# A scan that starts from the tile of the chunk before: one VectorE copy per chunk removed, two halves exchanged, one load moved

## The chip, the cores and the metric

The kernel runs on one core of a Trainium2 chip. The metric is the device time of one execution in microseconds (us). The core has a matrix engine (PE, with its weight loads shown apart as PEld), VectorE (DVE), ScalarE (ACT), GpSimd (POOL), and a queue of SyncE (SP) that only issues DMA transfers here. Each engine takes its own instructions in order; between engines, and between an engine and a DMA, waits go through semaphores.

## The reference

The input is eight images of 128 x 128 points with 128 channels. A first layer (linear attention with a residual) and the front of a second (a projection to 256 channels, a 3x3 depthwise convolution, SiLU) are not touched by the change. What matters is the selective scan after them. For four directions of walking over an image (rows, rows backwards, columns, columns backwards), and for each of the 256 channels and 16384 points in walking order:

```python
def step(xc, inp):
    dlt, dut, Bt, Ct = inp
    dA = jnp.exp(dlt[..., None] * A[:, None])
    xc = dA * xc + dut[..., None] * Bt[:, :, None, :]
    y = jnp.einsum('kbcn,kbn->kbc', xc, Ct)
    return (xc, y)
```

The state has one number per channel, so `y = xc * C`. The four directions are brought back to natural order and added up, gated with SiLU(z), normalized over the channels and projected to 128 channels.

## The kernel before

The program has three stages, one after the other: `layer0`, `layer1_front` and `layer1_scan`. Only `layer1_scan` is changed. It begins about 4870 us after the start.

**Units.** The output images are handled one after the other, eight in all. Each has four sweeps (a `Slot`; its `place` is 0 to 3), one for each direction, and each sweep is cut into 16 chunks of 1024 points. One chunk of one sweep is a unit: there are 512, numbered by n. The 256 channels stand in two halves c = 0, 1 of 128 partitions, so that a unit's data are a tile `ubt` of 128 x 2 x 1024 fp32 numbers (1 MB), loaded from DRAM by `load(n)`. There are four such buffers.

**Work on a unit.** `delta` (PE) makes the step sizes in a PSUM tile `px`, `soften` (ACT) takes their softplus into `sp`, `decay` (ACT) the exponential back into `px`, `weigh` (POOL) multiplies `ubt` by `sp` in place. `scan` (VectorE, L899 backwards and L901 forwards) runs the recurrence over the 1024 points of each channel half, in place in `ubt`. Its starting value is a pointer to a column of a small tile `state`, or 0.0 for the first chunk of a sweep. `state` (L909) fills that tile: a VectorE reduction with one element per channel, that is, a copy of the last element of each half of `ubt` (column 1023, or column 0 when the sweep walks backwards). `spread` (PE) makes C in PSUM for each half of 512 points.

**Adding up.** The sum over directions stands in a big SBUF tile `y`. In a sweep of place 0, `emit` (L927) writes h * C straight into `y`, in two halves of 512 points. In places 1 to 3, `emit` for the first half writes h * C into PSUM (L939, L943), `gather` (L951) adds that to `y`, and `emit` for the second half multiplies `ubt` in place (L932); POOL adds that half to `y` in `add` (L958). Once `emit` has overwritten a half of `ubt`, the scan's own value is gone from it, which is why the state is copied.

**Order.** `step(n)` writes out the order of all engines by hand, and the context `in_order` keeps it. On VectorE, one step is: emit, gather and emit of unit n-1, then `scan(n, 0)`, `scan(n, 1)`, `state(n)`. During the place-0 sweep of images 1 to 7, the image before leaves as well ("leaving"): two gates (multiplications with z, one on VectorE, one on POOL, L978), squares, moments and projection (PE), `variance` (L1011) behind `state`, and `store` (L1029), eight small VectorE instructions between the two scans that fill two buffers `r`; each `r` goes out by a 256 KB DMA of SP (L1033). In the same steps and those around them, POOL starts DMAs that add a 1 MB block of DRAM to `y` (L854).

**Queue of SP.** In a place-0 step it issues, in this order: four small loads of `rows` for unit n+2 (L863, L864), `load(n + 3)` (L870), two loads of z (L974) and the two stores of `r` (L1033). In places 1 to 3 `load(n + 3)` stands at the end of the step. `load(n + 3)` overwrites the buffer of unit n-1, so it waits until that has been read for the last time: by `emit(n - 1, 1)` in place 0, by `add(n - 1)` in the others.

Of the kernel before, what the change touches and what calls it, by code (L numbers as in the profile page):

```python
# [8 lines left out]
F32 = mybir.dt.float32  # L9
BF16 = mybir.dt.bfloat16  # L10
AF = mybir.ActivationFunctionType
ALU = mybir.AluOpType
AX = mybir.AxisListType
# [3 lines left out]
P = 128  # L17
B = 8
H = W = 128
L = H * W  # L20
NH, HD = 4, 32
NC2 = 2
# [8 lines left out]
CH = 1024  # L31
CW = CH // H
NCH = L // CH
# [664 lines left out]
def layer1_scan(ctx: ExitStack, tc, ubs, xps, zs, gs, dtw, dtb, a_log, gamma, beta, w_out, out):  # L698
# [15 lines left out]
    nc = tc.nc  # L714
# [3 lines left out]
    sm = ctx.enter_context(tc.tile_pool(name="l2s", bufs=4))  # L718
# [34 lines left out]
    for i in range(3):  # L753
        t = const.tile([P, CH], BF16, name=f"rows{i}")
# [3 lines left out]
    for i in range(3):  # L758
        t = const.tile([P, D2], BF16, name=f"dtw{i}")
# [20 lines left out]
    for j in range(2):  # L780
        for hf in range(2):
            at = 32 * (2 * j + hf)
# [19 lines left out]
    class Slot:  # L802


        def __init__(self, n, o, s):
            self.o, self.s = o, s
            self.b, self.k = o // 4 + 2 * s, o % 4
            self.back = self.k % 2 == 1
            self.order = NAT if self.k >= 2 else TURN
            self.dt_image, dt_dir = 2 * self.k + self.b // 4, self.b % 4  # L810
            self.dt_order = NAT if dt_dir >= 2 else TURN
            self.dt_turned_back = self.back != (dt_dir % 2 == 1)
            self.y_turned = (self.order == TURN) != (s >= 2)
            self.y_back = s % 2 == 1
            self.place = n % K
            self.dw = dws[n % 3]

        def weights(self):
# [24 lines left out]
    units = []  # L843
    for o in range(B):
        for s in ([3, 0, 1, 2] if o % 4 < 2 else [1, 2, 3, 0]):
            sl = Slot(len(units) // NCH, o, s)
            units += [(sl, i) for i in range(NCH)]

    ubt, sp, da, st = {}, {}, {}, {}

    def add_d(o, m):

# [3 lines left out]
    def load_rows(n):  # L856
        sl, i = units[n]
        m = sl.at(i)
        rw = rws[n % 3]
        md = NCH - 1 - m if sl.dt_turned_back else m  # L860
        src = xps[sl.dt_image, sl.dt_order].rearrange("j r l -> (j r) l")
        for j in range(3):
            nc.sync.dma_start(rw[3 * NR * j : 3 * NR * j + 3 * NR, :], src[:, md * CH : md * CH + CH])  # L863
        nc.sync.dma_start(rw[96:99, :], xps[sl.b, sl.order, :, R + 1, m * CH : m * CH + CH])  # L864

    def load(n):
        sl, i = units[n]
        m = sl.at(i)
        ubt[n] = wp.tile([P, NC2, CH], F32, name="ubt", tag="ub", bufs=4)
        nc.sync.dma_start(ubt[n], ubs[sl.b, sl.order].rearrange("c p l -> p c l")[:, :, m * CH : m * CH + CH])  # L870
# [16 lines left out]
    def decay(n, c):  # L887
        sl, i = units[n]
        nc.scalar.activation(da[n, c], sp[n, c], AF.Exp, scale=sa[:, sl.s, c : c + 1])  # L889
# [4 lines left out]
    def scan(n, c):  # L894
        sl, i = units[n]
        x, e = da[n, c], ubt[n][:, c, :]
        start = 0.0 if i == 0 else st[n - 1][:, c : c + 1]
        if sl.back:
            nc.vector.tensor_tensor_scan(e[:, ::-1], x[:, ::-1], e[:, ::-1], start, ALU.mult, ALU.add)  # L899
        else:  # L900
            nc.vector.tensor_tensor_scan(e, x, e, start, ALU.mult, ALU.add)  # L901

    def state(n):
        sl, i = units[n]
        st.pop(n - 1, None)
        if i < NCH - 1:
            st[n] = t = sm.tile([P, NC2], F32, name="state")
            at = 0 if sl.back else CH - 1
            nc.vector.tensor_reduce(t, ubt[n][:, :, at : at + 1], AX.X, ALU.max)  # L909

    cps, ts = {}, {}

    def spread(n, hf, tag):
        cps[n, hf] = p = pe.tile([P, 1, GN], F32, name="pc", tag=tag)
        nc.tensor.matmul(p[:, 0, :], csel, rws[n % 3][:, hf * 512 : hf * 512 + 512], start=True, stop=True)  # L915

    def emit(n, hf):

        sl, i = units[n]
        h = ubt[n][:, :, hf * 512 : hf * 512 + 512]
        c = cps.pop((n, hf)).to_broadcast([P, NC2, GN])
        if sl.place == 0:
            v = sl.y_at(i, hf)
            split = "p c (a b) -> p c a b"
            nc.vector.tensor_tensor(v, h.rearrange(split, b=H), c.rearrange(split, b=H), ALU.mult)  # L927
            if hf == 1:
                ubt.pop(n)
            return  # L930
        if hf == 1:
            nc.vector.tensor_tensor(h, h, c, ALU.mult)  # L932
            return
        p = da.pop((n, 1))
        if sl.y_turned:
            ts[n] = p.rearrange("p (c b a) -> p c b a", c=NC2, a=GW)
            t = p.rearrange("p (c b a) -> p c a b", c=NC2, a=GW)
            split = "p c (a b) -> p c a b"
            nc.vector.tensor_tensor(t, h.rearrange(split, b=H), c.rearrange(split, b=H), ALU.mult)  # L939
        else:  # L940
            t = p.rearrange("p (c q) -> p c q", c=NC2)
            ts[n] = t.rearrange("p c (a b) -> p c a b", b=H)
            nc.vector.tensor_tensor(t, h, c, ALU.mult)  # L943

    def gather(n):

        sl, i = units[n]
        v = sl.y_at(i, 0)
        if sl.y_turned:
            v = v.rearrange("p c a b -> p c b a")  # L950
        nc.vector.tensor_tensor(v, v, ts.pop(n), ALU.add)  # L951

    def add(n):
        sl, i = units[n]
        h = ubt.pop(n)[:, :, 512:].rearrange("p c (a b) -> p c a b", b=H)
        v = sl.y_at(i, 1)
        for c in range(NC2):
            nc.gpsimd.tensor_tensor(v[:, c], v[:, c], h[:, c], ALU.add)  # L958

# [10 lines left out]
    def fetch(o, m):  # L970
        for hf in range(2):
            zt[m, hf] = z = wp.tile([P, NC2, GN], F32, name="z", bufs=6)
            p = mirrored(o, m, hf)
            nc.sync.dma_start(z, zs[o].rearrange("c p l -> p c l")[:, :, p * GN : p * GN + GN])  # L974

    def gate(o, m, hf, eng):
        z, ym = zt[m, hf], piece(m, hf)
        eng.tensor_tensor(z, ym[:, :, ::-1] if o % 2 == 1 else ym, z, ALU.mult)  # L978

    def square(m, hf):  # L980
        nc.scalar.activation(piece(m, hf), zt[m, hf], AF.Square)  # L981
# [57 lines left out]
    for o in range(B):  # L1039
        n = (o + 1) * K * NCH  # L1040
# [11 lines left out]
    N = len(units)  # L1052

    def step(n):
        live = 0 <= n < N
        then = n + 1 < N
        before = 1 <= n <= N
        now, last, soon, later = (leaving.get(n + i) for i in (0, -1, 1, 2))
        first = before and units[n - 1][0].place == 0
        if before:  # L1060
            emit(n - 1, 0)
            if not first:
                gather(n - 1)
        if now and last:
            gate(*now, 1, nc.vector)
        if before:
            emit(n - 1, 1)
        if n + 2 < N:
            load_rows(n + 2)
        if first and n + 3 < N:  # L1070
            load(n + 3)
        if n in fetched:
            fetch(*fetched[n])
        if live:
            decay(n, 0)
        if now:
            square(now[1], 1)
        if live:
            decay(n, 1)
            weigh(n, 0)  # L1080
        if last:
            deviation(last[1])
        if live:
            weigh(n, 1)
        if now:
            moments(now[1])
        if live:
            scan(n, 0)
            da.pop((n, 0))
        if last:  # L1090
            for hf in range(2):
                store(*last, hf)
        if then:
            for c in range(NC2):
                delta(n + 1, c)
        if now:
            keep(now[1])
        if then:
            soften(n + 1, 0)
        if now:  # L1100
            to_tokens(now[1])
            square_mean(now[1])
        if then:
            soften(n + 1, 1)
        if live:
            scan(n, 1)
            state(n)
        if now:
            variance(now[1])
        if live:  # L1110
            spread(n, 0, "pc")
            spread(n, 1, "pt")
        if soon and now:
            gate(*soon, 0, nc.gpsimd)
        elif soon:
            gate(*soon, 1, nc.gpsimd)
        elif later:
            gate(*later, 0, nc.gpsimd)
        if soon:
            square(soon[1], 0)  # L1120
        if now:
            p = da.pop((n, 1)) if live else px.tile([P, CH], F32, name="px")
            for hf in range(2):
                project(now[1], hf, p[:, hf * 512 : hf * 512 + 512])
        elif live and units[n][0].place == 0:
            da.pop((n, 1))
        if before and not first:
            add(n - 1)
        if n + 3 < N and not first:
            load(n + 3)  # L1130
        if n in weighed:
            units[weighed[n]][0].weights()
        if n in summed:
            add_d(*summed[n])
# [78 lines left out]
```

## Time and profile before

| what | value |
|---|---|
| time, median of 3 runs | 9600.28 us (9591.18 to 9600.95) |
| profiled execution: its time, and its span | 9596.25 us, 9594.5 us |
| VectorE busy | 8167.1 us, 85% of the span |
| POOL, ACT, PE busy | 7188.9 us, 7164.4 us, 6323.6 us |
| both scan lines with a state pointer | 480 + 480 instructions, 2336 ns each, 2211 us |
| `state`, L909 | 480 instructions, 155 ns each, 74.5 us |
| `ubt` loads, L870 | 512 DMAs of 1 MB |

A group of instructions in the profile has its line, engine and operation, the tiles it writes and reads, the shapes and the count; behind the first bar the busy time and the mean time of one; behind the second the engine's idle time before them, with what ended most of it. Busy times of VectorE overlap: an instruction that waits for nothing begins some 80 ns before the end of the one in front, so the pitch from start to start, not the duration, says what an instruction costs. Durations and waits are those of the profiled execution.

### The profile page before, as it was taken

Reading aid. Unit: us, or ns where it says so; the run is one execution under the profiler, and the core shown is the slowest. Engines: PE = TensorE matmul, PEld = TensorE weight load, DVE = VectorE, ACT = ScalarE, POOL = GpSimd, SP = SyncE. Lnnn points to the kernel's source line nnn. Section 1 sums busy time; section 2 is a strip of 40 time slices with the busy share of each in tenths; the row PEclk is TensorE's granted clock in tenths of the full one; section 3 lists DMA queues with packets and bytes.
Section 4 is the critical chain, followed back from the end, with each engine's and each line's share of the span. In section 5 each row is a group of like instructions: output and inputs, shape, how many; then the busy total and the mean of one; then the engine's idle time right before and its main releaser. Section 6 shows DMA issues by size and latency. Waiting matters only on the chain. (4 is left out here: it accounts for less than half of the span.)

```text
span 9594.5 us, 89820 instructions
## 1 busy us (share of the span) xinstructions
PE 6323.6 (66%) x24190; PEld 3144.2 (33%) x24352; DVE 8167.1 (85%) x8668; ACT 7164.4 (75%) x8256; POOL 7188.9 (75%) x4361
## 2 busy tenths in 40 slices
PE   8999998988977788777823544636345363543636
PEld 5555655554322233222300311304023040220403
DVE  6667765563988899888989999999999999999996
ACT  5556565566877788777878888887887888788785
POOL 3445544455665578776859999998998999999897
PEclk9999999999988899888955755757556575665857
DMA  2332233313476678987765957769486685867858
GB/s 91 133 133 83 92 132 132 132 75 135 172 262 233 227 262 248 266 264 265 248 199 166 271 164 216 229 177 263 150 237 203 185 259 164 242 190 198 242 165 212
DMA packets 1034807, 1851.21 MB, mean 193 GB/s; under 512 B 274852, under 2 KB 500772, under 8 KB 1026112
## 3 DMA queue, kind: packets, MB, share of 16 engines
q1 hardware_dynamic: 999488, 1711.23, 54.2%
q0 software_dynamic: 34816, 134.23, 7.1%
q8 instruction: 199, 3.26, 0.1%
q14 instruction: 304, 2.49, 0.1%
HBM read 1153.03 MB, written 692.12 MB: 192 GB/s over the span
## 5 line engine op out<-in xcount | busy, mean ns | idle before, releaser
L892 POOL TENSOR_TENSOR ubt<-ubt,sp 128x1024 f32<-128x1024 f32 x1024 | 2457.5, 2456 | 197.3 <-ACT sp L885 107.8
L881 PE MATMUL px<-rows,dtw 128*128 128x512 bf16 x1893 | 914.6, 576 | 2259.8 <-DVE y L951 1032.6
L516 POOL TENSOR_TENSOR tap<-tap 128x1024 f32<-128x1024 f32 x512 | 1206.0, 2366 | 634.7 <-ACT tap L514 511.8
L524 DVE SCALAR_TENSOR_TENSOR acc<-xb,cw,acc 128x1024 f32<-128x1024 f32 x1024 | 1320.7, 1290 | 52.7 <-ACT tap L514 0.9
L885 ACT ACTIVATE sp<-px 128x1024 f32<-128x1024 f32 x1024 | 1044.2, 1024 | 398.3 <-PE px L881 244.5
L958 POOL TENSOR_TENSOR y<-y,ubt 128x512 f32<-128x512 f32 x768 | 1164.2, 1568 | 138.0 <-DVE ubt L932 135.1
L506 PE MATMUL acc<-xi,wt 128*128 128x512 f32 x2048 | 953.9, 609 | 384.6 <-ACT ures L531 384.2
L881 PEld LDWEIGHTS <-dtw 128*128 128x128 bf16 x2048 | 164.8, 110 | 3054.1 <-issue 951.5
L889 ACT ACTIVATE px<-sp,sa 128x1024 f32<-128x1024 f32 x1024 | 1110.2, 1109 | 6.1
L899 DVE TENSOR_TENSOR_SCAN ubt<-px,state,ubt 128x1024 f32<-128x1024 f32 x480 | 1106.2, 2336 | 6.6 <-issue 4.9
L901 DVE TENSOR_TENSOR_SCAN ubt<-px,state,ubt 128x1024 f32<-128x1024 f32 x480 | 1105.0, 2336 | 6.5 <-issue 4.7
L514 ACT ACTIVATE tap<-xb,cw 128x1024 f32<-128x1024 f32 x768 | 834.0, 1139 | 68.4 <-POOL tap L516 67.9
L885 ACT ACT_TABLE_LOAD x512 | 656.9, 1283 | 185.3 <-PE px L881 149.8
L282 POOL TENSOR_TENSOR q<-q,qs 128x512 f32<-128x512 f32 x256 | 271.2, 1060 | 642.2 <-DVE qs L281 642.2
L506 PEld LDWEIGHTS acc<-xi,wt 128*128 128x128 f32 x2048 | 383.9, 192 | 929.8 <-ACT ures L531 486.7
L889 ACT ACT_TABLE_LOAD x512 | 656.9, 1283 | 9.1
L1023 PEld LDWEIGHTS px<-wg,z 128*128 128x128 f32 x4096 | 586.7, 229 | 132.2 <-issue 126.4
L1023 PE MATMUL px<-wg,z 128*128 128x128 f32 x4096 | 585.6, 312 | 0.0
L915 PE MATMUL pc<-rows,csel 128*128 128x512 bf16 x1017 | 516.3, 588 | 100.8 <-DVE rstd L1011 91.8
L479 PE MATMUL pxb<-xi,wi 128*128 128x512 f32 x1024 | 495.9, 606 | 4.3 <-ACT xb L488 4.3
L951 DVE TENSOR_TENSOR y<-y,px 128x1024 f32<-128x1024 f32 x384 | 468.6, 1220 | 14.2
L298 ACT ACTIVATE sq<-o 128x512 f32<-128x512 f32 x256 | 161.2, 630 | 423.0 <-DVE o L296 421.8
(158 smaller groups left out, 15369.2 us busy)
## 6 DMA issues: line engine op xcount, KB each, us to landing
ubt<-ubs SPq DMA_DIRECT2D x512, 1024.0 KB
zs<-z SPq DMA_DIRECT2D x512, 256.0 KB
ubs<-ures SPq DMA_DIRECT2D x256, 512.0 KB
ubs<-turned SPq DMA_DIRECT2D x256, 512.0 KB
z<-zs SPq DMA_DIRECT2D x256, 512.0 KB
y<-gs POOLq DMA_DIRECT2D x128, 1024.0 KB, 12.0
rows<-xps SPq DMA_DIRECT2D x1536, 60.0 KB
xi<-x SPq DMA_DIRECT2D x120, 576.0 KB
```

What stands on the lines that cost most here:

```text
L506: nc.tensor.matmul(acc[:, s, :], wt[:, j, c, :], x, start=(j == 0), stop=(j == len(ON_PE) - 1))
L514: nc.scalar.activation(t, at(n, c, *d), AF.Copy, scale=cw[:, c, tap(*d) : tap(*d) + 1])
L516: nc.gpsimd.tensor_tensor(sums[n, c], sums[n, c], t, ALU.add)
L524: nc.vector.scalar_tensor_tensor(acc, at(n, c, *d), cw[:, c, tap(*d) : tap(*d) + 1], acc, ALU.mult, ALU.add)
L881: nc.tensor.matmul(p[:, hf * 512 : hf * 512 + 512], sl.dw[:, c * P : c * P + P], src, start=True, stop=True)
L885: nc.scalar.activation(t, da[n, c], AF.Softplus)
L889: nc.scalar.activation(da[n, c], sp[n, c], AF.Exp, scale=sa[:, sl.s, c : c + 1])
L892: nc.gpsimd.tensor_tensor(ubt[n][:, c, :], ubt[n][:, c, :], sp.pop((n, c)), ALU.mult)
L899: nc.vector.tensor_tensor_scan(e[:, ::-1], x[:, ::-1], e[:, ::-1], start, ALU.mult, ALU.add)
L901: nc.vector.tensor_tensor_scan(e, x, e, start, ALU.mult, ALU.add)
L958: nc.gpsimd.tensor_tensor(v[:, c], v[:, c], h[:, c], ALU.add)
L1023: nc.tensor.matmul(po[:, w, :], z[:, c, w * H : w * H + H], wg[:, c, :], start=(c == 0), stop=(c == NC2 - 1))
```

## The change

Four edits that belong together. The scan's starting value is now read from `ubt` of the unit before, at its last element, so `state` and its tile go. That element must then survive until `scan(n, 1)`: the half of `ubt` that holds it must not be overwritten in place, so in places 1 to 3 of a forward sweep the halves change roles: half 1 goes through PSUM and `gather`, half 0 is multiplied in place and added by POOL (`first` is the number of the half that goes to PSUM). In backward sweeps the last element is in half 0, and nothing is exchanged. The order of `emit` and of `spread` follows. Finally the buffer of unit n-1 is free later: in a place-0 step `load(n + 3)` moves behind `scan(n, 1)`, and so behind the z loads and the two stores in SP's queue; in the others it stays at the end of the step and waits for `scan(n, 1)` besides `add(n - 1)`.

```diff
+            self.first = 1 if self.place and not self.back else 0
...
     def scan(n, c):
-        start = 0.0 if i == 0 else st[n - 1][:, c : c + 1]
+        last = 0 if sl.back else CH - 1
+        start = 0.0 if i == 0 else ubt[n - 1][:, c, last : last + 1]
...
-    def state(n):
-        sl, i = units[n]
-        st.pop(n - 1, None)
-        if i < NCH - 1:
-            st[n] = t = sm.tile([P, NC2], F32, name="state")
-            at = 0 if sl.back else CH - 1
-            nc.vector.tensor_reduce(t, ubt[n][:, :, at : at + 1], AX.X, ALU.max)
...
     def emit(n, hf):
-            if hf == 1:
-                ubt.pop(n)
             return
-        if hf == 1:
+        if hf != sl.first:
             nc.vector.tensor_tensor(h, h, c, ALU.mult)
             return
...
     def gather(n):
-        v = sl.y_at(i, 0)
+        v = sl.y_at(i, sl.first)
...
     def add(n):
-        h = ubt.pop(n)[:, :, 512:].rearrange("p c (a b) -> p c a b", b=H)
-        v = sl.y_at(i, 1)
+        hf = 1 - sl.first
+        h = ubt[n][:, :, hf * 512 : hf * 512 + 512].rearrange("p c (a b) -> p c a b", b=H)
+        v = sl.y_at(i, hf)
...
     def step(n):
-            emit(n - 1, 0)
+            half1 = units[n - 1][0].first
+            emit(n - 1, half1)
...
-            emit(n - 1, 1)
+            emit(n - 1, 1 - half1)
         if n + 2 < N:
             load_rows(n + 2)
-        if first and n + 3 < N:
-            load(n + 3)
...
             scan(n, 1)
-            state(n)
+        if first:
+            ubt.pop(n - 1)
+            if n + 3 < N:
+                load(n + 3)
...
-            spread(n, 0, "pc")
-            spread(n, 1, "pt")
+            half1 = units[n][0].first
+            spread(n, half1, "pc")
+            spread(n, 1 - half1, "pt")
...
         if before and not first:
             add(n - 1)
+            ubt.pop(n - 1)
```

More of the change, by code (lines that the diff above doesn't have):

```diff
@@ L847, in layer1_scan @@
             units += [(sl, i) for i in range(NCH)]
-    ubt, sp, da, st = {}, {}, {}, {}
+    ubt, sp, da = {}, {}, {}
     def add_d(o, m):
```

## The prediction

> **What bounds the kernel now.** I read the page's totals first, then VectorE's waits in the scan stage, its timeline where a sweep ends, and the timelines of VectorE and SP where it stalls.
>
> ```profile
> PE 6323.6 (66%) x24190; PEld 3144.2 (33%) x24352; DVE 8167.1 (85%) x8668; ACT 7164.4 (75%) x8256; POOL 7188.9 (75%) x4361
> L909 DVE TENSOR_REDUCE state<-ubt 128x2 f32<-128x2 f32 x480 | 74.5, 155 | 16.5
> ```
>
> VectorE is the busiest engine, and in the scan stage it is 95% busy (4502.55 of 4724 us in the window from 4870 us). What the change removes looks like 91 us there: 480 copies with 74.5 us of busy time and 16.5 us of idle time before them. Whether that is real is seen at the last chunk of a sweep, where no copy is made. VectorE's timeline has such a chunk behind an ordinary one:
>
> ```profile
> 5680.47 4.58 DVE L899 TENSOR_TENSOR_SCAN ubt<-px,state,ubt 128x1024 f32<-128x1024 f32 x2
> 5685.09 0.15 DVE L909 TENSOR_REDUCE state<-ubt 128x2 f32<-128x2 f32 x1
> 5685.16 1.22 DVE L939 TENSOR_TENSOR px<-ubt,pc 128x1024 f32<-128x1024 f32 x1
> 5686.42 1.22 DVE L951 TENSOR_TENSOR y<-y,px 128x1024 f32<-128x1024 f32 x1
> 5687.55 1.21 DVE L932 TENSOR_TENSOR ubt<-ubt,pc 128x1024 f32<-128x1024 f32 x1
> 5688.69 4.58 DVE L899 TENSOR_TENSOR_SCAN ubt<-px,state,ubt 128x1024 f32<-128x1024 f32 x2
> 5693.37 1.23 DVE L939 TENSOR_TENSOR px<-ubt,pc 128x1024 f32<-128x1024 f32 x1
> 5694.64 1.22 DVE L951 TENSOR_TENSOR y<-y,px 128x1024 f32<-128x1024 f32 x1
> 5695.77 1.21 DVE L932 TENSOR_TENSOR ubt<-ubt,pc 128x1024 f32<-128x1024 f32 x1
> 5696.90 4.46 DVE L899 TENSOR_TENSOR_SCAN ubt<-px,ubt 128x1024 f32<-128x1024 f32 x2
> ```
>
> From scan to scan it is 8.22 us with the copy (5680.47 to 5688.69) and 8.21 without (5688.69 to 5696.90). The scans end at 5685.05 and 5693.27; with a copy, emit starts 0.11 us after that, without one 0.10. The first instruction that reads the scan's result has to wait for its end. If that is the copy, its own pitch of 0.07 us covers the rest of emit's start; if it is emit, which waits for VectorE and for PE, it starts that much later by itself. Over all chunks of places 1 to 3 the median period is 8.213 us with and 8.221 us without a copy. The copy is hidden.
>
> The stalls of VectorE are elsewhere. Its waits from 4870 to 9451 us, the longest in total first:
>
> ```profile
> DVE r L1029 <- DMA out<-r: 38.0, 25, 3.4
> DVE ubt L901 <- POOL ubt L892: 19.6, 5, 14.4
> DVE rstd L1011 <- ACT mv L1007: 16.1, 35, 1.5
> ```
>
> All 25 of the first row are in place-0 steps: the store wants a buffer `r` whose DMA of a step ago has not landed. The longest one, on VectorE and then in SP's queue:
>
> ```profile
> 7233.23 2.33 DVE L901 TENSOR_TENSOR_SCAN ubt<-px,state,ubt 128x1024 f32<-128x1024 f32 x1
> 7238.98 2.16 DVE L1029 SCALAR_TENSOR_TENSOR r<-px,rstd,bw 128x128 f32<-128x128 f32 x8 [3.42 <-DMA out<-r]
> ```
>
> ```profile
> 7222.24 0.38 SPq L870 DMA_DIRECT2D ubt<-ubs  x1
> 7222.73 1.02 SPq L974 DMA_DIRECT2D z<-zs  x2
> 7225.40 1.41 SPq L1033 DMA_DIRECT2D out<-r  x2
> ```
>
> The stores issued at 7225.40 stand behind 1 MB of `ubt`, issued 3.2 us earlier. In the packet records of this stretch the 4096-byte packets of `ubt` run until 7228, those of z until about 7230, and the 512-byte ones of the stores begin then. At 7231 POOL's accumulating DMA starts, takes about 45 packets per us until 7237, and the store ends only with it.
>
> **The skill.** The Trainium skill, "VectorE: DVE Perf Modes", section "The DRAIN you can't avoid", says that a read after a write on the same engine needs a semaphore, and that a semaphore costs nothing extra there. The trace agrees with the first and not with the second: an instruction without such a wait starts about 83 ns before the end of the one in front, the copy 34 ns after the scan's end, and emit, when it waits itself, 104 ns after it. "DMA: Bandwidth & Descriptors", section "Queues, rings and completion order", says that descriptors of a ring are taken in order and that an engine alternates between rings packet by packet. The packet records above agree. "SBUF — State Buffer", section "SBUF: two separate sides", has a VectorE operation with two SBUF inputs and a GpSimd one exclude each other: the gate (L978) takes 1.2 us or about 2.2 us, the longer where it overlaps a `weigh`.
>
> **The change part by part.** Copies, places 1 to 3: 8 images x 3 sweeps x 15 = 360, each +8 ns (8.221 - 8.213): +3 us. Copies in place 0 of images 1 to 7, 105 of them: `variance`, which does not read the scan, stands behind the copy. With a copy, the pitches of second scan, copy, `variance` and emit are 2374 + 73 + 73 + 1128 = 3648 ns; at the sweep's last chunk, without a copy, those of scan, `variance` and emit are 2257 + 186 + 1138 = 3581. That is -67 ns, -7 us in all, if VectorE bounds those steps. Image 0's 15 in place 0 have no `variance`: nothing.
>
> The pointer: the scan reads one column per channel half as before; 2336 ns with a pointer against 2281 without, so nothing changes. The exchange of halves: the same shapes, counts and neighbours on VectorE, PE and POOL: nothing; if the addresses mattered, it would show in 180 forward steps at most.
>
> The load in places 1 to 3: it is issued when `add(n - 1)` ends, 1.1 us (median) before the second scan ends (1.8 in place 3), so it goes out that much later. Behind it in SP's queue are the next step's `rows` loads, which wait for `spread` on PE and come about 0.7 us later, a whole step before they are used. The least time between a `ubt` landing and its `weigh` is 5.5 us in the records. Nothing; without that cover each us late would be a us on the path.
>
> The load in place 0 moves by 6.6 us (median; 10.1 at most), past two z loads and two stores. It landed 5.8 us after issue (median; 9.3 at most), and `weigh` came at least 16.8 us after that in images 1 to 7, 12.4 in image 0, where the move is 4.5 us. At least 6.7 us of margin remains. The stores now have only z and the `ubt` of the step before ahead of them. The 1 MB that leaves their way is 256 packets at 159 ns over 16 engines, 2.5 us, and up to 6 us at the rate left beside POOL's DMA. The stalls are 0.3 to 3.4 us, so most should go.
>
> What that is worth: 23 steps with such a stall last 13.06 us on average, the other 75 of chunks 1 to 14 last 11.14 (from scan starts). 23 x 1.92 = 44 us; this counts the waits that follow a stall (0.4 us for `mv`, 0.6 before the next scan) and the gate, which is mostly the short one after a stall. I take 70% of it, -31 us, since the 16 DMA engines are busy for 0.91 to 0.93 of all these sweeps, so other queueing will remain; the ends are 0 and all of 44. The 28 us of the same wait after 9451 us stay: there are no `ubt` loads any more.
>
> Sum: +3 - 7 - 31 = -35 us. The profiled execution took 9596.25 us (span 9594.5), the median is 4 us above. From 9600 that gives 9565 us.
>
> **The rivals.** (a) Likeliest, as above: 9540 to 9581, chance 0.64. (b) The stores are late for another reason (their own 512-byte packets, POOL's DMA), and only the copies' +3 and -7 us remain: 9596, within 0.2%. For it speaks that the three sweeps whose stores go out in 512-byte packets (images 3, 4, 7) hold 16 of the 23 stalled steps; against it that `ubt` packets are seen in front of the store. 0.20. (c) The copies were on the path after all: emit, waiting itself, starts as early as the copy did. Then 480 x 73 ns = 35 us more go, and 9530 results, or 9474 if all 91 us of the row went. The last chunks of all sweeps speak against it. 0.05. (d) Slower. The transfers of SP's queue use eight completion semaphores in turn, and a transfer waits for the one eight places ahead of it. With nine transfers in a place-0 step, the second store now waits for the `ubt` load of the step before to land; before, the last `rows` load did. The store comes about 8 us after that load's issue. While a load lands within 8 us it costs nothing; at the 9.3 us seen at most, plus 2 us of landing, the store is late by some 3 us, and so is `r`. If this happened in a third of the 105 steps, 35 x 3 = +105 us, less the 35 gained: 9670; at 20 steps it about balances. Slower by over 0.2%: 0.11.
>
> **How the numbers follow.** 0.2% (19 us) is about what a measurement of this kernel can tell from no change. Faster: (a) and (c), 0.69; same 0.20; slower 0.11. The range takes in all but (c)'s larger end and (d): 9535 to 9606; the likeliest case's own is 9540 to 9581.
>
> **What would show it.** Right: periods in places 1 to 3 of 8.22 us, emit starting 0.10 us behind the scan; the wait of `r` for its store down from 38 to about 10 us before 9451 us; place-0 sweeps of images 3, 4 and 7 down from 188.1, 191.6 and 186.0 us to about 180; no new wait of `weigh` for `ubt`. Wrong: periods near 8.14 us (c); the same waits of `r` (b); the second store held by a `ubt` landing, or longer gates because POOL now collides with them (d).

## The result

The changed kernel takes 9560.44 us (median of 6 runs, 9557.33 to 9567.8) against 9591.68 us of the kernel before (6 runs, 9581.65 to 9600.95). The ratio is 0.9968, with a 95% interval of 0.9957 to 0.9979: faster by 0.32%, or 31 us. The prediction said 9565 us, and faster.

The page of the changed kernel, its totals by engine and the group of one of the two scan lines:

```profile
PE 6331.1 (66%) x24352; PEld 3113.6 (33%) x24352; DVE 8131.2 (85%) x8188; ACT 7168.0 (75%) x8256; POOL 7193.5 (75%) x4361
L904 DVE TENSOR_TENSOR_SCAN ubt<-px,ubt 128x1024 f32<-128x1024 f32 x512 | 1176.5, 2330 | 25.4 <-POOL ubt L894 19.6
```

VectorE has 480 instructions fewer (8668 to 8188), but its busy time falls by only 36 us, not by the 74.5 us of the row that went: of a copy's 155 ns, the last 83 lay under the start of emit, and 480 x 72 ns is 35 us. The scans that start from a column of `ubt` cost what they did with a pointer to `state`: 2334 ns, 2336 before (the 2330 of the line has the 32 in it that start from 0.0).

The timeline of VectorE at the place where the copy was seen to be hidden, a chunk of places 1 to 3:

```profile
5674.97 4.58 DVE L902 TENSOR_TENSOR_SCAN ubt<-px,ubt 128x1024 f32<-128x1024 f32 x2
5679.66 1.23 DVE L932 TENSOR_TENSOR px<-ubt,pc 128x1024 f32<-128x1024 f32 x1
...
5683.19 4.58 DVE L902 TENSOR_TENSOR_SCAN ubt<-px,ubt 128x1024 f32<-128x1024 f32 x2
```

No copy, and from scan to scan still 8.22 us (5674.97 to 5683.19). The scan ends at 5679.55 and emit begins 0.11 us later, as it did behind the copy. The median over all chunks of places 1 to 3 is 8.221 us; it was 8.213 with the copy.

The waits of VectorE between 4870 and 9415 us, where the last scan ends:

```profile
DVE r L1023 <- DMA out<-r: 29.3, 17, 3.9
DVE ubt L904 <- POOL ubt L894: 19.6, 5, 14.5
DVE rstd L1005 <- ACT mv L1001: 17.1, 23, 1.7
```

The first row was 38.0 us in 25 waits. It fell by much less than the prediction took for its mechanism, and yet the time came out as predicted. Where the time went is seen in the seven sweeps of place 0 in which an image leaves. From first scan to first scan of the next sweep they took 175.6, 179.5, 188.1, 191.6, 180.1, 181.6 and 186.0 us, in all 1282.4; now 176.0, 176.9, 179.8, 181.6, 178.5, 178.7 and 179.2, in all 1250.8. That is -31.7 us, most of it where the prediction saw it, in images 3, 4 and 7, for which it had forecast about 180. The whole scan stage, first scan to last, became 29.5 us shorter, so everything outside these sweeps became some 2 us longer; the prediction had +3 us for places 1 to 3. (The profiled execution is 36.8 us shorter than that of before, since the two stages ahead, which nobody touched, ended 6.7 us earlier in it.)

The waits of SP's queue in the scan stage show the two things that the change added there, waits for the scan and for a landed `ubt`:

```profile
SPq L872 <- DVE ubt L904: 1025.5, 195, 7.7
...
SPq L1027 <- DMA ubt<-ubs: 173.5, 68, 5.3
```

The last row is the rival (d) of the prediction: 68 times the queue stood at the second store, for up to 5.3 us, until the `ubt` load of the step before had landed. Counted from when the store's `r` was full, 60 stores went out late for it, by 2.2 us on average. Before, the row had one wait, of 0.9 us. The mechanism exists, then; whether it costs anything is the question of one of the experiments.

### The profile page after: what moved, and what is told of

Read it like the earlier page. It is cut to its first block, busy times and chain, and to the rows that moved or that the text cites. A ratio compares the mean times of both kernels' runs of the same rounds, so it can differ in the third digit from the quotient of the medians.

```text
span 9557.7 us, 89859 instructions
## 1 busy us (share of the span) xinstructions
PE 6331.1 (66%) x24352; PEld 3113.6 (33%) x24352; DVE 8131.2 (85%) x8188; ACT 7168.0 (75%) x8256; POOL 7193.5 (75%) x4361
## 5 line engine op out<-in xcount | busy, mean ns | idle before, releaser
L883 PE MATMUL px<-rows,dtw 128*128 128x512 bf16 x2048 | 952.9, 565 | 2234.3 <-DVE y L944 1062.6
L904 DVE TENSOR_TENSOR_SCAN ubt<-px,ubt 128x1024 f32<-128x1024 f32 x512 | 1176.5, 2330 | 25.4 <-POOL ubt L894 19.6
L902 DVE TENSOR_TENSOR_SCAN ubt<-px,ubt 128x1024 f32<-128x1024 f32 x512 | 1178.0, 2331 | 12.3 <-POOL ubt L894 6.1
L1017 PEld LDWEIGHTS px<-wg,z 128*128 128x128 f32 x4096 | 560.5, 220 | 118.8 <-issue 113.7
L1017 PE MATMUL px<-wg,z 128*128 128x128 f32 x4096 | 560.8, 303 | 0.0
```

The source lines that it names most:

```text
L883: nc.tensor.matmul(p[:, hf * 512 : hf * 512 + 512], sl.dw[:, c * P : c * P + P], src, start=True, stop=True)
L1017: nc.tensor.matmul(po[:, w, :], z[:, c, w * H : w * H + H], wg[:, c, :], start=(c == 0), stop=(c == NC2 - 1))
```

## Experiments

Theory 1: the moved load is the whole gain, because 1 MB leaves the way of the stores. Rivals: the gain is in the copies; or the stores are late by themselves and the loads' place is indifferent.

### The moved load alone

The kernel before, with its copies and its halves; in a place-0 step the load goes behind the second scan. It still waits only for `emit`, so that it is issued as soon as the two stores ahead of it are.

```diff
         if n + 2 < N:
             load_rows(n + 2)
-        if first and n + 3 < N:
-            load(n + 3)
...
             scan(n, 1)
             state(n)
+        if first and n + 3 < N:
+            load(n + 3)
```

> The kernel before with one edit: in place-0 steps the load of unit n+3 stands behind the stores in SP's queue; the copies and the halves stay. Theory 1 (the moved load is what saves, because the stores no longer stand behind 1 MB): 15 to 30 us less than the kernel before, place-0 sweeps of images 1 to 7 near 180 us, waits of r for its store below 38 us. Theory 2 (the copies are what saves): no change, 0 to -5 us, sweeps as before.

Measured: 9552.59 us, ratio 0.9964 (0.9950 to 0.9977) to the 9588.11 us of the kernel before beside it. For the gain, no copy has to go and no halves have to change roles. VectorE's wait of `r` for its store, to the end of the last scan:

```profile
DVE r L1029 <- DMA out<-r: 17.2, 10, 2.8
```

The sweeps of place 0 come to 1243.2 us, even below the changed kernel's 1250.8.

### The rest of the change alone

The changed kernel in places 1 to 3, and place 0 as before: the copy kept there, and the load ahead of the stores.

```diff
-        start = 0.0 if i == 0 else ubt[n - 1][:, c, last : last + 1]
+        start = 0.0 if i == 0 else ubt[n - 1][:, c, last : last + 1] if sl.place else st[n - 1][:, c : c + 1]
...
+        if first:
+            ubt.pop(n - 1)
+            if n + 3 < N:
+                load(n + 3)
         if n in fetched:
             fetch(*fetched[n])
```

> The changed kernel with the copy kept in place 0 and the load there at its old spot; in places 1 to 3 no copy and the halves exchanged. Theory 1: the 360 copies were hidden, +3 us against the kernel before, periods of 8.221 us, emit 104 ns behind the scan. Theory 2: 360 x 73 ns = 26 us less. The same run bounds what exchanging the halves and the later load in places 1 to 3 do: nothing by theory 1.

Measured: 9589.98 us, ratio 1.0002 (0.9994 to 1.0011). The 360 copies, the exchanged halves and the later load of places 1 to 3 are worth nothing, and rival (c) falls. Its wait of `r` is 43.1 us in 28 waits, its sweeps of place 0 come to 1272.4 us.

### A second copy

If one copy is hidden under emit's start, a second one should not be. The kernel before with the reduction done twice, its second result unread.

```diff
             nc.vector.tensor_reduce(t, ubt[n][:, :, at : at + 1], AX.X, ALU.max)
+            t2 = sm.tile([P, NC2], F32, name="state2", bufs=1)
+            nc.vector.tensor_reduce(t2, ubt[n][:, :, at : at + 1], AX.X, ALU.max)
```

> The kernel before with a second copy of the state behind the first, which nothing reads. Theory 1 (one copy fills the time that emit would need anyway after the scan's end): the second one costs its whole pitch, 73 ns x 480 = +35 us, periods of 8.286 us in places 1 to 3. If a copy is free whatever stands there (VectorE not the bound): 0 us. If a copy costs its busy time: +74 us.

Measured: 9609.26 us, ratio 1.0027 (1.0018 to 1.0036), +26 us. VectorE's timeline:

```profile
5667.29 4.58 DVE L899 TENSOR_TENSOR_SCAN ubt<-px,state,ubt 128x1024 f32<-128x1024 f32 x2
5671.91 0.16 DVE L909 TENSOR_REDUCE state<-ubt 128x2 f32<-128x2 f32 x1
5671.98 0.15 DVE L911 TENSOR_REDUCE state<-ubt 128x2 f32<-128x2 f32 x1
5672.05 1.22 DVE L941 TENSOR_TENSOR px<-ubt,pc 128x1024 f32<-128x1024 f32 x1
```

Emit now starts 0.18 us behind the scan's end at 5671.87, and the median period is 8.275 us against 8.213: the second copy costs 62 ns, most of its pitch of 70. The first is free, the second is paid. That settles why the busy time of the copies was worth nothing in places 1 to 3.

### The load between z and the stores

If it is the stores that must not stand behind 1 MB, then moving the load behind the z loads only, still ahead of the stores, gains nothing. The kernel before with:

```diff
-        if first and n + 3 < N:
-            load(n + 3)
         if n in fetched:
             fetch(*fetched[n])
+        if first and n + 3 < N:
+            load(n + 3)
```

> The kernel before with the load of a place-0 step moved only half of the way: behind the two z loads, still ahead of the two stores. Theory 1 (what counts is 1 MB in the ring ahead of the stores): nothing gained, within 10 us of the kernel before, waits of r for its store 30 us or more. Rival (what counts is that z lands earlier, or that the load comes later at all): most of the gain of the load moved the whole way, some 30 us.

Measured: 9651.44 us, ratio 1.0059 (1.0046 to 1.0072) to 9592.52 us: not the same but 59 us slower. The waits of 30 us or more came, the time within 10 us did not; the rival's gain did not come either. The waits of VectorE from 4870 to 9400 us, and one row of SP's there:

```profile
DVE r L1029 <- DMA out<-r: 76.3, 40, 4.6
```

```profile
SPq L870 <- DMA out<-r: 83.7, 36, 5.4
```

The wait of `r` doubles, 38 to 76 us, and the sweeps of place 0 last 1348.5 us. Two things changed. The load goes out a median of 1.6 us ahead of the next store (3.5 us in the kernel before). And, two transfers further back in the queue, it now has the semaphore of a store of the step before, so that a store that is late makes the load late (36 times), which then stands still closer in front of the next stores. How the 59 us divide between the two was not told apart. What is shown is that the load's place, with the transfer that it comes to wait for, sets the wait in both directions, and that neither issuing z sooner nor issuing the load later is a help by itself.

### Without POOL's DMA

Theory 1 names a second partner: POOL's accumulating DMA, beside which the stores' 512-byte packets crawl. The kernel before without the call of `add_d`, load and copies as they were.

```diff
-        if n in summed:
-            add_d(*summed[n])
```

> The kernel before without POOL's accumulating DMAs: the D term of the sum is left out, and with it 128 DMAs of 1 MB and POOL's 1.28 us for each. If the stores are late only where such a DMA shares the engines with the 1 MB ahead of them: waits of r for its store before the last sweep below 3 us instead of 38, and place-0 sweeps of images 1 to 7 near 168 us (16 steps of 10.4 to 10.5 us). If the ubt load in front is enough by itself: waits of 15 us or more remain.

Measured: 9479.95 us, ratio 0.9883 (0.9868 to 0.9898). VectorE's waits from 4870 to 9340 us have no row of `r` for a store left at all; at the top is now

```profile
DVE rstd L1011 <- ACT mv L1007: 24.5, 22, 3.2
```

with sweeps of 1200.0 us. The 1 MB in front of the stores is therefore not enough for a stall; it takes POOL's DMA as well. With that DMA and the load behind the stores, 10 of 25 waits were left. (The kernel gains more than the wait, because the gates too get shorter: 158.2 us of VectorE in these sweeps, not 185.7.)

### The store off the load's semaphore

For rival (d), and for the 29.3 us that remain: the changed kernel with its two z loads merged into one. With eight transfers in a step, no longer nine, a store's place in the round of eight semaphores is no longer that of the `ubt` load.

```diff
+        z = wp.tile([P, NC2, 2, GN], F32, name="z", bufs=3)
         for hf in range(2):
-            zt[m, hf] = z = wp.tile([P, NC2, GN], F32, name="z", bufs=6)
-            p = mirrored(o, m, hf)
-            nc.sync.dma_start(z, zs[o].rearrange("c p l -> p c l")[:, :, p * GN : p * GN + GN])
+            zt[m, hf] = z[:, :, mirrored(o, m, hf) % 2, :]
+        p = min(mirrored(o, m, 0), mirrored(o, m, 1))
+        nc.sync.dma_start(z.rearrange("p c h g -> p c (h g)"), zs[o].rearrange("c p l -> p c l")[:, :, p * GN : p * GN + 2 * GN])
```

> The changed kernel with the two 256 KB z loads of a step as one of 512 KB, in three buffers of twice the size, so that SP's queue has eight transfers in a place-0 step and the second store no longer takes the completion semaphore of the last ubt load. If that semaphore is what keeps the waits of r for its store at 29 us (before 9415 us) where about 10 were forecast: 5 to 20 us less than the changed kernel, waits of r near 10 us, no wait of a store for a ubt load. If the stores are late because the 16 DMA engines are full: the same time as the changed kernel within 5 us.

Measured: 9573.65 us, ratio 0.9987 (0.9980 to 0.9993), by the two ratios some 18 us slower than the changed kernel, and a miss. The row of stores waiting for `ubt` is gone from SP's waits, but the wait of `r` is 36.3 us in 24, and the queue has a new row:

```profile
SPq L872 <- DMA ubt<-ubs: 118.0, 58, 4.1
```

Now a `ubt` load takes the semaphore of the one of the step before, and the one z load waits for both halves' projections. So a wait of `r` of this size comes about without a store that waits for a load; but to take that wait away by the number of transfers puts another in its place, and what the shared semaphore alone costs the changed kernel this run does not tell. Which of the two new waits makes this kernel slower was not told apart. (The sizes in the expectation are half of what they should be: the profile has 512 KB for each z load, so the two of a step are 1 MB, which stands ahead of the stores in every one of these kernels.)

### The load right behind the stores, in the changed kernel

The changed kernel has a longer wait of `r` than the load moved alone. One difference is that without a copy its load waits for the end of the second scan as well. The changed kernel with the copies kept in place 0 and the load behind them:

```diff
+    def state(n):
...
+        if i < NCH - 1 and sl.place == 0:
...
             scan(n, 1)
+            state(n)
         if first:
             ubt.pop(n - 1)
             if n + 3 < N:
                 load(n + 3)
```

> The changed kernel with the copy of the state kept in place 0 alone, so that the load there waits for emit only and goes out right behind the two stores, as in the run that moved only the load; places 1 to 3 stay as changed. Theory A: the changed kernel's wait of r for its store (29 us against 17 us in that run) is longer because its load waits for the end of the second scan and so goes out later, nearer to the next step's stores. Then the wait falls to about 17 us, the seven place-0 sweeps last about 1243 us in all (1250.8 in the changed kernel), and the kernel takes 5 to 10 us less than the changed one, about 0.9962 of the kernel before. Theory B: the wait of r is set by something else in the changed kernel, and the copies of place 0 cost their pitch: the wait stays near 29 us, the sweeps come to about 1260 us, and the kernel is 7 to 15 us slower than the changed one, about 0.998.

Measured: 9556.8 us, ratio 0.9965 (0.9951 to 0.9978) to 9592.48 us. That is 3.6 us less than the changed kernel, less than these intervals can tell. The profile says more:

| sweeps of place 0, images 1 to 7, us | before | changed | load alone | this one |
|---|---|---|---|---|
| in all | 1282.4 | 1250.8 | 1243.2 | 1244.5 |
| `r` waiting for its store (times) | 38.0 (25) | 29.3 (17) | 17.2 (10) | 25.1 (9) |
| all idle times over 0.15 us | 77.1 | 58.4 | 41.2 | 47.8 |
| pitches of scans, copy and `variance` | 543.3 | 528.7 | 539.4 | 538.7 |
| pitches of the gates | 185.7 | 188.2 | 188.9 | 183.8 |
| pitches of emit and store | 476.4 | 475.6 | 473.8 | 474.2 |

With copies and the load right behind the stores, the sweeps take 1243 to 1245 us, as theory A said. Without copies, their row is lower (by 10 us against this kernel, 14.6 against before), and the idle times are higher by 10 to 17 us. In part that is the same time under another name: where `variance` has to wait for ACT's `mv` anyway, the time that a copy had filled becomes idle. The wait of `r` itself did not fall to 17 us, as A had it: three kernels with this place-0 code (the last is below) show 17.2, 25.1 and 14.8 us, in 10, 9 and 8 waits. The number of waits holds from profile to profile, the microseconds in this one row don't.

### One wait less in emit

What bounds places 1 to 3 is emit's start behind the scan. In the trace, emit there waits for two things, the scan on VectorE and `spread` on PE, and a semaphore instruction of its own stands ahead of it. The changed kernel with `spread` done before the second half of the next `delta` on PE, and the wait for it put on `scan(n, 1)`, which has time for it (except in steps where an image leaves):

```diff
         if then:
-            for c in range(NC2):
-                delta(n + 1, c)
+            delta(n + 1, 0)
+        if live and not now:
+            half1 = units[n][0].first
+            spread(n, half1, "pc")
+            spread(n, 1 - half1, "pt")
+            seen.append(tc.nc.cur_bb.bb.instructions[-1])
+        if then:
+            delta(n + 1, 1)
...
             scan(n, 1)
+            for i in seen:
+                info = mybir.DependencyInfo(mybir.DependencyClass.Sync, mybir.DependencyReason.DATA)
+                tc.add_manual_dep(tc.nc.cur_bb.bb.instructions[-1], i.name, info, reason="c_ready")
...
-        if live:
+        if live and now:
             half1 = units[n][0].first
```

> The changed kernel, but outside of leaving steps spread stands on PE before the second half of delta, and scan(n, 1) carries the wait for it, so that the emit behind the scan waits for VectorE alone. If emit's 104 ns behind the scan's end are the time of two waits one after the other: 34 ns, periods in places 1 to 3 of 8.15 us instead of 8.221, and 375 x 70 ns = 26 us less than the changed kernel. If they belong to the operation (its PSUM operands) and not to the waits: 104 ns stay, no change.

Measured: 9537.45 us (9529.43 to 9539.42), ratio 0.9941 (0.9928 to 0.9953). VectorE's timeline:

```profile
5668.14 4.58 DVE L902 TENSOR_TENSOR_SCAN ubt<-px,ubt 128x1024 f32<-128x1024 f32 x2
5672.76 1.23 DVE L932 TENSOR_TENSOR px<-ubt,pc 128x1024 f32<-128x1024 f32 x1
...
5676.29 4.58 DVE L902 TENSOR_TENSOR_SCAN ubt<-px,ubt 128x1024 f32<-128x1024 f32 x2
```

Emit starts 0.04 us behind the scan's end at 5672.72, and the period is 8.15 us. Same arithmetic, one wait fewer on the instruction that the path runs through: 70 ns in some 375 chunks, 26 us. By the two ratios it is 26 us less than the changed kernel, and from first scan to last the profile has 4512.6 us, not 4538.9.

The two last edits together:

> The same with the earlier run's edit of the waits of emit added: the projection of C ahead of the second half of the next step sizes on PE, its wait carried by the second scan. If the gains of the two edits lie in different places (place 0, and places 1 to 3 with image 0), they add up: 26 us less than the run beside it, periods in places 1 to 3 of 8.15 us, about 0.9935 of the kernel before under theory A, and no better than 0.995 under theory B.

Measured: 9524.55 us (9523.58 to 9533.19), ratio 0.9935 (0.9922 to 0.9947), the fastest kernel of the study: 32 us below the run beside it, where 26 were expected, with a period of 8.15 us. The sweeps of place 0 were 1239.6 us.

## Why the prediction was right

**Copies in places 1 to 3, +3 us.** Right. The period went from 8.213 to 8.221 us as read off the last chunks before; the run with this part alone is at 1.0002, and that with a second copy shows that only what goes beyond emit's own start is paid.

**Copies in place 0, -7 us.** Right, in size too, for the stretch that it looked at. From the start of the second scan to the end of emit's pitch it is 3653 ns on average in the kernel before (the 70 of 105 steps in which VectorE waits for nothing there) and 3580 in the changed kernel (81 steps): 73 ns, where 67 were predicted, some 6 us in all. The 14.6 us of the table's row are no measure of it, since the run with the load alone has 3.9 us of them with all copies in place, and in the other steps the copy's time became waiting. That the kernel is faster for it is not shown: beside the run that kept these copies, with its load right behind the stores, it is no faster.

**Pointer, halves, load in places 1 to 3: nothing.** Right. The scans take 2334 ns; the run with these parts in place and place 0 untouched shows no difference. The least time from a landing of `ubt` to its `weigh` is 5.0 us there, and in place 0, images 1 to 7, 8.6 us (predicted: at least 6.7). POOL has no new wait for `ubt`.

**The load in place 0, -31 us.** The mechanism was right, the term's working was not. Shown right: the load alone gives the gain (0.9964), the load closer to the stores loses 59 us, and without POOL's DMA the wait is gone. Shown wrong: "from 38 to about 10 us". It is 29.3 us. The term was 70% of the 44 us by which the 23 steps with a stall outlast the others. There are 14 such steps now, of 13.16 us against 10.95 for the others, which makes 31 us: 13 us of the 44 went, not 31. What made up for it was not forecast: steps without a stall became shorter, 11.14 to 10.95 us in the mean, 18.6 us in 98 steps. At most 6 of these can be the copies'; the runs that moved the load and kept the copies have it as well (10.96 and 10.89 us). In idle times, 8.7 us of this wait went and 10 us of others in the same steps (`r` waiting for PE or POOL 9.4 to 1.4 us, the next scan for issue 12.4 to 2.8, less 7.4 us in which a scan now waits for ACT's `decay`). That the sum came out is luck to this extent: the step of the working that was to give -31 us gave 13, and a shortening that it had put at nothing gave most of the rest.

**What kept the wait at 29 us.** The prediction took it that the load is out of the stores' way once it is behind them. It is then ahead of the stores of the next step. SP's timeline around one of the longest stalls that remain, and VectorE's:

```profile
6618.85 0.37 SPq L872 DMA_DIRECT2D ubt<-ubs  x1
...
6622.24 1.54 SPq L968 DMA_DIRECT2D z<-zs  x2
6626.76 4.12 SPq L1027 DMA_DIRECT2D out<-r  x2
```

```profile
6639.95 2.16 DVE L1023 SCALAR_TENSOR_TENSOR r<-px,rstd,bw 128x128 f32<-128x128 f32 x8 [3.06 <-DMA out<-r]
```

In the packet records POOL's DMA runs from 6619.7 to 6629.0 us. The load issued at 6618.85 has its first packets at 6622.2, gets some 30 of them per us beside it and ends at 6629.7; z follows until about 6632. VectorE waits for the buffer of the first store, issued at 6626.76: its packets begin at 6631.7 and run into POOL's next DMA (6632.4 to 6639.4), and it has landed at 6639.8. The chain is as before, with the load stretched over the step's border. That fits the counts: with the load right behind the stores there are 8 to 10 waits in three profiles; the changed kernel and the one with one wait less, whose loads wait for the scan, have 17 and 24. The course of this one stall is read from the records, not shown by a run.

The counts fit a second account too. Six of the changed kernel's 17 waits (16.1 us) are for the buffer of the first store. The other eleven (13.2 us) are for that of the second, and in all eleven the second store had been held until the `ubt` load landed. The kernel with one wait less has 18 such waits, the three with the load right behind the stores 4, 3 and 6. But a store that was held is not yet a store that is late for it: in the five of the eleven in images 4 and 7, its packets follow those of the first store with no gap over 20 ns, so the queue lost nothing by holding it. For the other six this stays open.

**The rivals.** (b), 9596: fell, the load's place decides. But its parts were no fiction: without POOL's DMA there is no wait. (c): fell. (d): the wait is there, 68 times and 2.6 us on average, more often than the break-even of about 20 steps; but the step from a late store to a late `r` failed for most: 49 of the 60 stores that went out late made no `r` late, and the wait of `r` fell all the same. What the other eleven owe to it is open, as said. **The tail**: the wait of `r` after the last scan was to stay at 28.0 us; it is 31.6.

**Smaller readings of the prediction that the traces do not bear out.** In the kernel before, the second store took the semaphore of the first `rows` load of its own step, not of the last. A `ubt` load had landed 0.5 us after its last packet (median; 1.7 at most), not 2. POOL's DMA in the stall that it shows ended at 7238.3 us, not 7237. And a gate that overlaps a `weigh` is not always a long one: 57 of the 59 long gates start while a `weigh` runs, but so do 19 of the 61 short ones. None of these changes the sum.

The Trainium skill, "DMA: Bandwidth & Descriptors", section "Queues, rings and completion order", which the prediction used for the order in a ring and the turns between rings, fits the runs with the load ahead of the stores and behind them (38 against 17 us of waits) and the one without POOL's DMA (none).

## What to carry to other kernels

Before you count the instructions that a change removes, look at where one of them is missing already: the last chunk of a sweep gave the answer for the copies, and a doubled copy the proof. Do not take a sum that comes out for a proof of its terms. Put the transfers that something waits for ahead of the large ones that nobody waits for yet, in the same queue, as early behind them as the buffers allow; and check the next step's transfers too. When an instruction on the path waits for two engines, see whether an earlier instruction can take one of the waits.

## What the runs showed of the hardware

- A VectorE instruction that waits for nothing begins 83 ns before the end of the one in front; one that waits for VectorE alone 34 ns after it; one with two waits, of which one is an instruction of its own, 104 ns after it. The Trainium skill, "VectorE: DVE Perf Modes", section "The DRAIN you can't avoid", has it that in a chain of copies on VectorE a semaphore costs nothing extra; no run here repeats that chain, but in these traces a first wait moves the start by 117 ns and a second one by 70 more, and the run that moves the second gains its 70.
- The same nine transfers of a step cost 59 us more with the load two places further back, and 35 us less with it four places back. In the first case it had come to wait for the landing of a store, 83.7 us in 36 waits: the queue's transfers use eight semaphores in turn in these traces, so that which transfer another one waits for depends on how many lie between them, not on their data.
- Beside POOL's accumulating DMA, the changed kernel's `ubt` loads of place 0 came down to 31 packets of 4096 bytes per us (median of the 14 with over 150 of POOL's packets beside them), where it is 56 with none. The longest took 13.0 us from issue to the last packet, 4.5 of them before its first packet; the median is 7.28.
